# Expert blocks of a decoder's routed layer: separate PSUM tiles, one product moved, a table split over four slots

## The chip, the cores and the metric

The kernel runs on one core of a Trainium2 chip. The metric is the device time of one execution in microseconds (us), lower is better. The profiles name the engines PE (TensorE's matmuls), PEld (its weight loads), DVE (VectorE), ACT (ScalarE), POOL (GpSimd) and SP (SyncE, which issues most loads).

## The reference

Two decoder layers over x of 32 batches x 100 rows x 256 columns, with a context of 361 rows a batch and 16 heads. Each sub-layer is followed by a residual and a layer norm:

```python
x = _layernorm(x + _L0_attn_ref(x, ...))            # self-attention, softmax
x = _layernorm(x + _L0_xattn_ref(x, ctx, ctx, distances, ...))   # cross-attention, bias -log(distance)
x = _layernorm(x + _L0_ffn_ref(x, ...))             # layer norm, quantised rows, rounded weights
x = _layernorm(x + _L1_attn_ref(x, ...))
x = _layernorm(x + _L1_xattn_ref(x, ctx, ctx, ...))
x = _layernorm(x + _L1_ffn_ref(x, ...))
```

The change is in the last one, a layer of 8 experts in which each of the 3200 rows takes one:

```python
logits = x_flat @ Wg + bg
probs = softmax(logits); assignments = argmax(probs)
h = gelu(x_flat @ W1[e] + b1[e])        # for the assigned expert e
out = probs[e] * (h @ W2[e] + b2[e])
```

## The kernel before

**Slots.** Both layers' attention is written as one list of slots, five to a batch (`SLOTS`). `at(slot, place, do)` puts work into a slot; `run_slots` goes through the slots in order and emits first the scores of the step two slots ahead, then at three places the turning of the next step's probabilities with the side work of that place, and last the sums. The engines' order is the order in which this is written; nothing is rearranged later.

**Expert blocks.** While the second layer's cross-attention runs, each row's expert is found and the row is written to a region of its expert in DRAM (`regions`, values, the probability and the row's place). The regions are then handled in 32 blocks of 128 rows (`BLOCKS`), each block of one expert. A table says where each block's rows begin and whose they are. A block takes these steps:

- load its rows (`load_rows_of_block`, L112) and its expert's first matrix with bias (`load_matrix_of_block`, L115), from SP's queue;
- `turn_rows` (L117): two transposes on TensorE (L119) and one copy to SBUF on ScalarE (L120);
- `first_matrix` (L122): eight matmul passes (L126), then two activations on ScalarE with the bias (L128);
- `second_matrix` (L130): the second product (L132) from weights that stay in SBUF (`shared`), in a bank of the pool `ps_r` (four banks);
- `share_and_residual` (L135): four DVE instructions, bias, share and residual, mean and variance (L138 to L142);
- on POOL `margin` (L145) and `scale` (L148, power -0.5), on DVE `shift_of` (L151), for two blocks at a time;
- a normalisation on ScalarE (L1035) and an indirect store of the rows from POOL's queue (L779, `store`).

**Six begun blocks.** Six of the 32 blocks (`BEGUN`) are begun ahead: after 24 of the 32 batches their table is made (`table_of_begun`, L823), SP reads it (`begun_rows`), and rows are turned and first products computed in the last slots of the attention. `BEGINNING` lists for each block the (slot, place) of the turning and of the first product. They stop short of Gelu (`AF.Identity`), because ScalarE still holds the table of functions of the attention. After the last slot comes the load of the Gelu table, `table_of_others` (L836, it counts rows per expert and makes the other blocks' table on DVE, with a matmul at L801), `end_begun` (L880, Gelu at L883 and the second product of the six blocks) and `sum_begun`.

The begun blocks' table is 16 DVE instructions behind one matmul: `blocks_of_experts` (L797: count of blocks and its running sum, L803 to L809), four instructions for the whole blocks per expert (L827 to L830), `write_table` (L812, up to the transpose L821) and three for the other blocks' table (L832 to L834). All of it is emitted at slot `last + 15`, which is 313, at place 1. In that region of slots the DVE also has each pair's maximum rows (L379) and subtraction (L382) of the self-attention, and the division of a cross-attention's output (L350, L352).

**The loop.** The other 26 blocks run in a pipelined loop (L1047 to L1079). Iteration i emits: the load of block i+10, the turning of block i+2, the first product of block i+1 (now with Gelu), the normalisation of block i-3, the second product and the sum of block i, then margin and scale or shift, and the store of block i-3. Rows have 16 buffers, first matrices 12, the turned rows in SBUF (`bxT`) and the hidden rows (`bhT`) two each. In PSUM, the turned rows of block i+2 go to bank i%2 and the first product of block i+1 to bank 2 + (i+1)%2 of one tile, `sc_blocks`, of four banks. It has the shape of the attention's tile of scores and comes from the same pool, `ps_s`:

```python
banks = score_banks("blocks")          # one [P, 4, 512] tile for all blocks
turn_rows(t, banks[:, i % 2, :NC2 * P]...)
first_matrix(t, banks[:, 2 + i % 2, :NC2 * P]..., AF.Gelu)
```

Of the kernel before, what the change touches and what calls it, by code (L numbers as in the profile page):

```python
# [10 lines left out]
F32 = mybir.dt.float32  # L11
I32 = mybir.dt.int32
AF = mybir.ActivationFunctionType
# [5 lines left out]
E = 8  # L19
# [13 lines left out]
BLOCKS_AT_MOST = E * PER_EXPERT + E - 1  # L33
FILLS = 23
BEGUN, BEGIN_WITH = 6, 24
BEGINNING = (((338, 1), (340, 2)), ((338, 3), (342, 1)), ((339, 1), (343, 3)), ((339, 3), (345, 2)), ((340, 1), (346, 0)), ((341, 1), (347, 1)))
NO_TOKEN = 1000000
ROUND = 12582912.0
AHEAD = range(2, 10)
# [27 lines left out]
def decoder_kernel(ctx: ExitStack, tc: tile.TileContext, a: dict, out: bass.AP):  # L67
# [85 lines left out]
    def centre_and_scale(dst, src, scale):  # L153
        nc.vector.tensor_scalar(dst, src, scale[0], scale[1], ALU.subtract, ALU.mult)

    ps_s = ctx.enter_context(tc.tile_pool(name="ps_s", bufs=1, space=bass.MemoryType.PSUM))
    ps_r = ctx.enter_context(tc.tile_pool(name="ps_r", bufs=4, space=bass.MemoryType.PSUM))

    def bank(tag):
        return ps_r.tile([P, 512], F32, tag="r", name=f"r_{tag}")  # L160

    def score_banks(tag):
        return ps_s.tile([P, NG, 512], F32, tag="s", name=f"sc_{tag}")

    with ExitStack() as att:
        w1 = att.enter_context(tc.tile_pool(name="w1", bufs=1))
        w2 = att.enter_context(tc.tile_pool(name="w2", bufs=2))
        sm = att.enter_context(tc.tile_pool(name="sm", bufs=4))
        att.enter_context(tc.manual_schedule())

        def split(t, n):
            return t.rearrange("p (n s) -> p n s", n=n)
# [285 lines left out]
        def at(slot, place, do):  # L458
            plan.setdefault((slot, place), []).append(do)
# [337 lines left out]
        def blocks_of_experts(name, offset, before):  # L797


            ps = bank(name)[:, :E]  # L800
            nc.tensor.matmul(ps, lhsT=share_of_block, rhs=sofar, start=True, stop=True)  # L801
            n = sm.tile([P, E], F32, tag="tb_n", name=f"{name}_n")
            nc.vector.tensor_scalar(n, ps, offset, ROUND, ALU.add, ALU.add)  # L803
            if before is None:
                nc.vector.tensor_scalar(n, n, ROUND, None, ALU.subtract)
            else:
                nc.vector.scalar_tensor_tensor(n, n, ROUND, before, ALU.subtract, ALU.subtract)
            upto = sm.tile([P, E], F32, tag="tb_upto", name=f"{name}_upto")
            nc.vector.tensor_tensor_scan(upto, ones[:, :E], n, 0.0, ALU.mult, ALU.add)  # L809
            return n, upto  # L810
# [12 lines left out]
        def table_of_begun():  # L823

            assert BEGIN_WITH * S - E * (P - 1) > (BEGUN - 1) * P
            n, upto = blocks_of_experts("begun", 0.5 / P - 0.5, None)
            nc.vector.tensor_scalar(upto, upto, float(BEGUN), None, ALU.min)  # L827
            nc.vector.tensor_copy(done[:, 0:1], upto[:, 0:1])
            nc.vector.tensor_tensor(done[:, 1:], upto[:, 1:], upto[:, :E - 1], ALU.subtract)
            nc.vector.tensor_scalar(n, done, -float(P), float(B * S), ALU.mult, ALU.add)  # L830
            write_table("begun", upto, lambda: n, c["steps"][:, 0:1])
            nc.vector.tensor_tensor(over, done[:, 1:], done[:, :E - 1], ALU.subtract)  # L832
            nc.vector.tensor_scalar(over, over, float(P), float(B * S), ALU.mult, ALU.add)
            nc.vector.scalar_tensor_tensor(first_done, done[:, 0:1], float(P), c["steps"][:, 0:1], ALU.mult, ALU.add)  # L834

        def table_of_others():  # L836

# [29 lines left out]
        def of_bank(name):  # L867
            return split(bank(name)[:, :NC2 * P], NC2)

        def plan_beginning():  # L870
            last = starts(1, BEGIN_WITH - 1)[0]
            at(last + 15, 1, table_of_begun)
            at(last + 22, 3, begun_rows)
            at(last + 48, 3, begun_experts)
            for i, (turning, first) in enumerate(BEGINNING):
                at(last + 23 + i, 0, lambda i=i: load_begun(i))
                at(*turning, lambda i=i: turn_rows(blocks[i], of_bank(f"bt_{i}")))
                at(*first, lambda i=i: first_matrix(blocks[i], of_bank(f"bh_{i}"), AF.Identity))

        def end_begun():  # L880

            for t in blocks[:BEGUN]:
                nc.scalar.activation(t["hT"], t["hT"], AF.Gelu)  # L883
                t["ps"] = bank("bo")[:, :D]
                second_matrix(t, t["ps"], shared)

# [103 lines left out]
    with ExitStack() as moe:  # L990
        mw = moe.enter_context(tc.tile_pool(name="mw", bufs=1))
        m2 = moe.enter_context(tc.tile_pool(name="m2", bufs=2))
        m4 = moe.enter_context(tc.tile_pool(name="m4", bufs=4))
        m16 = moe.enter_context(tc.tile_pool(name="m16", bufs=16))
        m12 = moe.enter_context(tc.tile_pool(name="m12", bufs=12))
        moe.enter_context(tc.manual_schedule())

        y_all = mw.tile([P, BLOCKS - BEGUN, D], F32, name="y_all")
        for i in range(BEGUN, BLOCKS):
            blocks[i]["y"] = y_all[:, i - BEGUN, :]  # L1000

        banks = score_banks("blocks")

        def load_block(i):
            n = min(4, BLOCKS - i)
            if (i - BEGUN) % 4 == 0:
                firsts = of_table(i - BEGUN, n, 0, (ENG.SP,), (BLOCKS_AT_MOST - 1) * P)
                experts = of_table(i - BEGUN, n, 1, (ENG.SP, ENG.PE, ENG.DVE), E - 1)
                for t, first, e in zip(blocks[i:i + n], firsts, experts):
                    t["first"], t["e"] = first, e  # L1010
            t = blocks[i]
            t["x"] = m16.tile([P, ROW], F32, tag="xb", name=f"xb_{i}")
            t["w"] = m12.tile([P, WROW], F32, tag="wb", name=f"wb_{i}")
            for load in (load_matrix_of_block, load_rows_of_block) if i == BEGUN else (load_rows_of_block, load_matrix_of_block):
                load(t)

        def turn_block(i):
            t = blocks[i]
            t["ident"] = ident
            t["xT"] = m2.tile([P, NC2, P], F32, tag="bxT", name=f"bxT_{i}")  # L1020
            turn_rows(t, banks[:, i % 2, :NC2 * P].rearrange("p (k s) -> p k s", k=NC2))

        def first_layer(i):
            t = blocks[i]
            t["hT"] = m2.tile([P, NC2, P], F32, tag="bhT", name=f"bhT_{i}")
            first_matrix(t, banks[:, 2 + i % 2, :NC2 * P].rearrange("p (k s) -> p k s", k=NC2), AF.Gelu)

        def second_layer(i):
            ps = bank(f"bo_{i}")[:, :D]
            second_matrix(blocks[i], ps, shared)  # L1030
            share_and_residual(i, ps, m4)

        def normalise_on_scalar(i):
            y = blocks[i]["y"]
            nc.scalar.activation(y, y, AF.Identity, bias=shift[:, i:i + 1], scale=rs_all[:, i:i + 1])  # L1035

        def normalise(i):
            y = blocks[i]["y"]
            centre_and_scale(y, y, (mv_all[:, i, 0:1], rs_all[:, i:i + 1]))

        def store(i):
            scatter("out", out=out.rearrange("b s d -> (b s) d"),
                    out_offset=bass.IndirectOffsetOnAxis(ap=blocks[i]["x"][:, D + 1:].bitcast(I32), axis=0), in_=blocks[i]["y"],
                    bounds_check=B * S - 1, oob_is_err=False)

        half = BEGUN // 2
        for i in range(BEGUN - 10, BLOCKS):  # L1047
            for f, d in ((load_block, 10), (turn_block, 2), (first_layer, 1)):
                if BEGUN <= i + d < BLOCKS:
                    f(i + d)  # L1050
            if i == BEGUN - 1:
                for j in range(half):
                    normalise_on_scalar(j)
                    store(j)
            if i < BEGUN:
                continue
            if i > BEGUN + 2:
                normalise_on_scalar(i - 3)
            second_layer(i)
            if i == BLOCKS - 1:  # L1060
                normalise_on_scalar(i - 2)
                store(i - 3)
            if i == BEGUN + 1:
                margin(half, half)
                scale(half, half)
            if i % 2:
                margin(i - 1, 2)
                scale(i - 1, 2)
            elif i > BEGUN:
                shift_of(i - 2, 2)  # L1070
            if BEGUN + 1 < i < BEGUN + 2 + half:
                normalise(i - 2 - half)
                store(i - 2 - half)
            if BEGUN + 2 < i < BLOCKS - 1:
                store(i - 3)
        store(BLOCKS - 3)
        for i in range(BLOCKS - 2, BLOCKS):
            normalise(i)
            store(i)  # L1079
# [70 lines left out]
```

## Time and profile before

| | us |
|---|---|
| median of 3 runs | 1764.14 (1762.48 to 1765.47) |
| profiled execution | 1761.08 |
| its span in the trace | 1759.0 |
| start of the six second products | 1659.50 |
| second product of block 7 / 29 | 1676.64 / 1740.25 |
| one block of the loop | 2.88 |

The mean granted TensorE clock of the profiled execution is 0.995 of full speed. Positions are microseconds from the start of the span. A row of a timeline has its start, its duration, engine, line, operation, output and input tiles, shape and count; a bracket behind it is the time that the engine stood idle ahead of it, and what ended that. Up to about 1657 the profile shows the attention and what is done beside it; the expert stage is the last 100 us.

### The profile page before, as it was taken

How to read it: one execution, taken by the hardware profiler on the slowest of the kernel's cores; microseconds unless marked ns; L12 is line 12 of the kernel's file. 1: busy time of each engine (PE TensorE's matmuls, PEld its weight loads, DVE VectorE, ACT ScalarE, POOL GpSimd, SP SyncE). 2: the span in 40 equal slices, each digit the busy share in tenths (PEclk: the TensorE clock that was granted, in tenths of full speed). 3: DMA queues.
4: the chain of work that ended last, by engine and by line, in shares of the span. 5: the costliest groups of instructions: out<-in, count | busy, mean ns of one | idle time of the engine just before them, and what ended most of it. 6: DMA issues, size and time to landing. Idle time of an engine off the chain costs nothing.

```text
span 1759.0 us, 52227 instructions
## 1 busy us (share of the span) xinstructions
PE 1689.9 (96%) x20803; PEld 1298.5 (74%) x20803; DVE 1295.7 (74%) x3803; ACT 913.0 (52%) x2255; POOL 1096.0 (62%) x1655
## 2 busy tenths in 40 slices
PE   8999999999999999999999999999999999999885
PEld 6677777777777777766777777777777777776664
DVE  5677777777777777777668787877777777867754
ACT  3455555555555555555445555555555555554443
POOL 1565666666666666666157777676767676675455
PEclk9999999999999999999999999999999999999998
DMA  4000331333133213200511131000001000120261
GB/s 159 14 25 27 81 84 46 82 81 83 49 84 81 77 51 84 76 25 22 186 44 55 55 107 60 13 26 19 20 18 28 19 26 13 44 81 13 70 217 41
DMA packets 64047, 104.90 MB, mean 60 GB/s; under 512 B 6107, under 2 KB 43485, under 8 KB 63678
## 3 DMA queue, kind: packets, MB, share of 16 engines
q1 hardware_dynamic: 59790, 94.44, 18.3%
q0 software_dynamic: 3584, 6.59, 1.2%
q8 instruction: 165, 2.70, 0.6%
q14 instruction: 76, 0.62, 0.1%
q10 hardware_dynamic: 432, 0.54, 0.1%
HBM read 61.32 MB, written 41.13 MB: 58 GB/s over the span
## 4 chain that ended last, share of the span: by engine, by line
PE 76%; DVE 15%; POOL 4%; issue 3%; DMA 1%; ACT 1%; SPq 0%; POOLq 0%; ACTq 0%; DVEq 0%
PE r_t_x L435 13%; PE sc_x L341 10%; PE r_k L536 8%; PE r_v L545 7%; PE r_a_x L450 6%; DVE pr L421 6%; PE r_t_s L392 4%; PE r_o_x L364 3%; POOL pr L425 3%; PE r_qx L321 2%; PE r_o_s L364 2%; PE sc_s L341 2%; PE r_a_s L399 2%; DVE pr_s L382 2%; DVE mx_s L379 2%
## 5 line engine op out<-in xcount | busy, mean ns | idle before, releaser
L425 POOL TENSOR_TENSOR pr<-pr,mx_x 100x361 f32<-100x361 f32 x992 | 766.2, 802 | 229.4 <-DVE mx_x L421 220.2
L436 ACT ACTIVATE pT_x<-r_t_x 120x400 f32<-120x400 f32 (+1 forms) x768 | 371.0, 503 | 269.5 <-PE r_t_x L435 267.2
L435 PEld LDWEIGHTS r_t_x<-ident,pr 100*120 100x120 f32 (+1 forms) x3072 | 313.8, 138 | 111.6 <-POOL pr L425 32.8
L435 PE MATMUL r_t_x<-ident,pr 100*120 100x100 f32 (+1 forms) x3072 | 380.8, 252 | 11.8 <-POOL pr L425 10.8
L421 DVE CUSTOM_DVE_ANT_0 pr<-sc_x,dist 100x361 f32<-100x361 f32 x512 | 244.7, 531 | 121.7 <-PE sc_x L341 97.7
L421 DVE CUSTOM_DVE_ANT_0 pr<-sc_x,zero 100x361 f32<-100x361 f32 x512 | 244.6, 530 | 76.4 <-PE sc_x L341 70.3
L341 PE MATMUL sc_x<-kT_x,qz_x 32*100 32x361 f32 x2048 | 221.8, 502 | 7.8 <-DVE mx_x L421 4.5
L96 POOL TENSOR_SCALAR rs_s<-mv_s 100x1 f32<-100x1 f32 x64 | 14.3, 223 | 292.3 <-DVE mv_s L94 261.7
L450 PE MATMUL r_a_x<-pT_x,v_cross 120*32 120x100 f32 (+1 forms) x6144 | 172.2, 252 | 0.0
L379 DVE TENSOR_REDUCE mx_s<-sc_s 100x16 f32<-100x1600 f32 x64 | 116.6, 1822 | 70.8 <-PE sc_s L341 70.8
L538 ACT ACTIVATE kT_x<-r_k,c_columns 128x361 f32<-128x361 f32 x128 | 72.0, 563 | 161.8 <-PE r_k L536 161.8
L450 PEld LDWEIGHTS r_a_x<-pT_x,v_cross 120*32 120x32 f32 (+1 forms) x6144 | 129.9, 110 | 24.4 <-ACT kT_s L485 2.2
L393 ACT ACTIVATE pT_s<-r_t_s 100x400 f32<-100x400 f32 x256 | 112.5, 504 | 28.8 <-PE r_t_s L392 26.3
L382 DVE TENSOR_TENSOR pr_s<-sc_s,mx_s 100x1600 f32<-100x1600 f32 x64 | 116.8, 1825 | 2.2
L392 PE MATMUL r_t_s<-ident,pr_s 100*100 100x100 f32 x1024 | 106.2, 249 | 0.3 <-DVE pr_s L382 0.3
L341 PEld LDWEIGHTS sc_x<-kT_x,qz_x 32*100 32x100 f32 x2048 | 68.2, 159 | 44.6 <-issue 16.1
L545 PE MATMUL r_v<-shared,ctx 128*120 128x256 f32 (+1 forms) x384 | 100.5, 384 | 0.0
L392 PEld LDWEIGHTS r_t_s<-ident,pr_s 100*100 100x100 f32 x1024 | 94.3, 129 | 5.5 <-ACT shared L547 0.6
L547 ACT COPY v_cross<-r_v 120x256 f32<-120x256 f32 x168 | 62.5, 372 | 58.0 <-PE r_v L545 58.0
L332 DVE SCALAR_TENSOR_TENSOR qz_x<-r_qx,qm_x_scale,qm_x_bias 128x400 f32<-128x400 f32 x64 | 37.6, 630 | 70.1 <-PE r_qx L321 70.1
L536 PE MATMUL r_k<-ctx,c_l1x_wk 128*128 128x361 f32 x256 | 89.1, 470 | 0.1
L536 PE MATMUL r_k<-ctx,shared 128*128 128x361 f32 x256 | 88.6, 468 | 0.0
(254 smaller groups left out, 2912.7 us busy)
## 6 DMA issues: line engine op xcount, KB each, us to landing
regions<-no_token SPq DMA_DIRECT2D x23, 1161.0 KB
ctx<-in_ctxT_dram SPq DMA_DIRECT2D x64, 361.0 KB
wb<-in_experts_dram SPq DMA_DIRECT2D x26, 257.0 KB
values_dram<-shared SPq DMA_DIRECT2D x8, 768.0 KB
v_cross<-values_dram SPq DMA_DIRECT2D x8, 768.0 KB
dist<-in_dist_dram SPq DMA_DIRECT2D x32, 141.0 KB
xb<-regions SPq DMA_DIRECT2D x26, 129.0 KB
x_all<-in_x_dram SPq DMA_DIRECT2D x32, 100.0 KB
```

The costliest lines, as they stand in the source:

```text
L341: nc.tensor.matmul(dst, lhsT=qz[rows, p, k, :], rhs=kT[rows, k, :], start=True, stop=True)
L379: nc.vector.tensor_reduce(mx, sg, AX.X, ALU.max)
L382: nc.vector.tensor_tensor(pr, sg, mx.unsqueeze(3).to_broadcast([S, NG, NG, S]), ALU.subtract)
L392: nc.tensor.transpose(pt[:, j, :], t["pr_s"][:, j, g, :], ident[:S, :S])
L393: nc.scalar.activation(t["pT_s"][:, g], pt, AF.Exp)
L421: nc.vector.tensor_tensor_reduce(pr[:, j, :SK], sc[:, j, :], bias, 1.0, LOWEST, ALU.add, ALU.max, mx)
L425: nc.gpsimd.tensor_tensor(pr[:, j, :SK], pr[:, j, :SK], mx.to_broadcast([S, SK]), ALU.subtract)
L435: nc.tensor.transpose(pt[:n, j, :], t["pr_x", g][:, j, k0:k0 + n], ident[:S, :S])
L436: nc.scalar.activation(t["pT_x", g][:n, i], pt[:n], AF.Exp)
L450: nc.tensor.matmul(av[32 * j:32 * j + 32, h, :], lhsT=t["v_x"][:n, i, head(part, j), :], rhs=t["pT_x", part][:n, i, j, :], start=(i == 0), ...
L536: nc.tensor.matmul(ps, lhsT=c[sx + "_wk"][:, k, m * P:(m + 1) * P], rhs=t["ctx"][:, k, :], start=(k == 0), stop=(k == NC2 - 1))
L545: nc.tensor.matmul(ps, lhsT=ctx_b[:, k, k0:k0 + n], rhs=c[sx + "_wv"][:, k, :], start=(k == 0), stop=(k == NC2 - 1))
```

## The change

Three things change; the instructions and their number stay.

1. In the loop, each block's turned rows and each block's first product get a PSUM tile of their own, of half a bank, from a new pool `ps_m` with two buffers for each of the two kinds. In the program as built these four tiles lie in four banks, where the one tile was. The pool of the scores is closed with the attention.
2. The first product of the sixth begun block (`BEGINNING[5]`), which had slot 347, place 1, is now written in `end_begun` behind the Gelu of the first block, ahead of the six second products. On TensorE it comes right behind the matmul of the counting (L801); on ScalarE its two biased copies come behind the first Gelu.
3. `table_of_begun` returns four parts (count, whole blocks, rows of the table, the part for the other blocks), which are put at place 3 of the slots 313 to 316 instead of all at place 1 of slot 313.

```diff
-BEGINNING = (..., ((340, 1), (346, 0)), ((341, 1), (347, 1)))
+BEGINNING = (..., ((340, 1), (346, 0)), ((341, 1), None))
...
-    ps_s = ctx.enter_context(tc.tile_pool(name="ps_s", bufs=1, space=bass.MemoryType.PSUM))
...
+        ps_s = att.enter_context(tc.tile_pool(name="ps_s", bufs=1, space=bass.MemoryType.PSUM))
...
         def table_of_begun():
-            n, upto = blocks_of_experts("begun", 0.5 / P - 0.5, None)
-            nc.vector.tensor_scalar(upto, upto, float(BEGUN), None, ALU.min)
...
+            u = {}
+            def counts():
+                u["n"], u["upto"] = blocks_of_experts("begun", 0.5 / P - 0.5, None)
+            def whole_blocks():
+                n, upto = u["n"], u["upto"]
+                nc.vector.tensor_scalar(upto, upto, float(BEGUN), None, ALU.min)
+                nc.vector.tensor_copy(done[:, 0:1], upto[:, 0:1])
+                nc.vector.tensor_tensor(done[:, 1:], upto[:, 1:], upto[:, :E - 1], ALU.subtract)
+                nc.vector.tensor_scalar(n, done, -float(P), float(B * S), ALU.mult, ALU.add)
+            def rows():
+                write_table("begun", u["upto"], lambda: u["n"], c["steps"][:, 0:1])
+            def for_others():
...
+            return counts, whole_blocks, rows, for_others
...
-            at(last + 15, 1, table_of_begun)
+            for i, part in enumerate(table_of_begun()):
+                at(last + 15 + i, 3, part)
...
-                at(*first, lambda i=i: first_matrix(blocks[i], of_bank(f"bh_{i}"), AF.Identity))
+                if first:
+                    at(*first, lambda i=i: first_matrix(blocks[i], of_bank(f"bh_{i}"), AF.Identity))
...
         def end_begun():
-            for t in blocks[:BEGUN]:
+            for i, t in enumerate(blocks[:BEGUN]):
                 nc.scalar.activation(t["hT"], t["hT"], AF.Gelu)
+                if i == 0:
+                    first_matrix(blocks[BEGUN - 1], of_bank("bh"), AF.Identity)
                 t["ps"] = bank("bo")[:, :D]
                 second_matrix(t, t["ps"], shared)
...
+        ps_m = moe.enter_context(tc.tile_pool(name="ps_m", bufs=2, space=bass.MemoryType.PSUM))
...
-        banks = score_banks("blocks")
...
-            turn_rows(t, banks[:, i % 2, :NC2 * P].rearrange("p (k s) -> p k s", k=NC2))
+            turn_rows(t, ps_m.tile([P, NC2, P], F32, tag="t", name=f"bt_{i}"))
...
-            first_matrix(t, banks[:, 2 + i % 2, :NC2 * P].rearrange("p (k s) -> p k s", k=NC2), AF.Gelu)
+            first_matrix(t, ps_m.tile([P, NC2, P], F32, tag="h", name=f"bh_{i}"), AF.Gelu)
```

More of the change, by code (lines that the diff above doesn't have):

```diff
@@ L35 @@
 BEGUN, BEGIN_WITH = 6, 24
-BEGINNING = (((338, 1), (340, 2)), ((338, 3), (342, 1)), ((339, 1), (343, 3)), ((339, 3), (345, 2)), ((340, 1), (346, 0)), ((341, 1), (347, 1)))
+BEGINNING = (((338, 1), (340, 2)), ((338, 3), (342, 1)), ((339, 1), (343, 3)), ((339, 3), (345, 2)), ((340, 1), (346, 0)), ((341, 1), None))
 NO_TOKEN = 1000000
@@ L160, in bank @@
         return ps_r.tile([P, 512], F32, tag="r", name=f"r_{tag}")
-    def score_banks(tag):
-        return ps_s.tile([P, NG, 512], F32, tag="s", name=f"sc_{tag}")
     with ExitStack() as att:
@@ L168, in decoder_kernel, with score_banks @@
         sm = att.enter_context(tc.tile_pool(name="sm", bufs=4))
+        ps_s = att.enter_context(tc.tile_pool(name="ps_s", bufs=1, space=bass.MemoryType.PSUM))
         att.enter_context(tc.manual_schedule())
+        def score_banks(tag):
+            return ps_s.tile([P, NG, 512], F32, tag="s", name=f"sc_{tag}")
         def split(t, n):
@@ L825, in table_of_begun @@
             assert BEGIN_WITH * S - E * (P - 1) > (BEGUN - 1) * P
-            n, upto = blocks_of_experts("begun", 0.5 / P - 0.5, None)
-            nc.vector.tensor_scalar(upto, upto, float(BEGUN), None, ALU.min)
[L828 to L834, printed above, removed]
+            u = {}
[10 more added lines that the diff above has]
+            def for_others():
+                nc.vector.tensor_tensor(over, done[:, 1:], done[:, :E - 1], ALU.subtract)
+                nc.vector.tensor_scalar(over, over, float(P), float(B * S), ALU.mult, ALU.add)
+                nc.vector.scalar_tensor_tensor(first_done, done[:, 0:1], float(P), c["steps"][:, 0:1], ALU.mult, ALU.add)
+            return counts, whole_blocks, rows, for_others
         def table_of_others():
```

## The prediction, written before the changed kernel ran

> **What bounds the kernel now.** One run is profiled: 1761.08 us, of which the span is 1759.0. I read the page's top first:
>
> ```profile
> PE 1689.9 (96%) x20803; PEld 1298.5 (74%) x20803; DVE 1295.7 (74%) x3803; ACT 913.0 (52%) x2255; POOL 1096.0 (62%) x1655
> ```
>
> TensorE is busy 96% over all stages, but the change is in one stage and one slot, so then TensorE's timeline in the expert loop and where the loop starts, then the chain, ScalarE's timeline and the turned rows' tile to see who holds whom. In the loop one block is three rows, each ring closing with the next block's L132:
>
> ```profile
> 1720.10 1.03 PE L132 MATMUL r_bo<-shared,bhT 128*128 x4
> 1721.03 0.44 PE L119 MATMUL sc_blocks<-ident,xb 128*128 128x128 f32 x2
> 1721.99 1.16 PE L126 MATMUL sc_blocks<-bxT,wb 128*128 128x128 f32 x8 [0.52 <-ACT bxT L120]
> 1722.98 1.03 PE L132 MATMUL r_bo<-shared,bhT 128*128 x4
> ```
>
> Start, duration, line, tiles; the bracket is TensorE's idle time before the row and what ended it. From second product to second product is 2.88 us. TensorE idles 0.52 of it, for ScalarE's copy of the rows that it has just turned. But the first product (L126) is that of block i+1 and the rows are those of block i+2: nothing it reads is late. All turned rows and first products live in one tile, so an access to one orders the next. ScalarE:
>
> ```profile
> 1720.35 0.62 ACT L128 ACTIVATE bhT<-sc_blocks,wb 128x128 f32<-128x128 f32 x2 [1.30 <-PE sc_blocks L126]
> 1720.87 0.60 ACT L1035 ACTIVATE y_all<-y_all,shift,rs_all 128x256 f32<-128x256 f32 x1
> 1721.56 0.37 ACT L120 COPY bxT<-sc_blocks 128x256 f32<-128x256 f32 x1
> ```
>
> The tile's own sum says that this is the usual case (us, times):
>
> ```profile
>   ACT bxT L120: 27.9, 44
>   PE sc_blocks L126: 22.1, 17
> ```
>
> The chain has the same ring in every block: 1.16 first product, 0.87 second, 0.35 turning, 0.38 copy. The other engines have room in 1716 to 1728 (12 us): DVE 6.62, ScalarE 6.11, POOL 6.46. Where the stage starts, TensorE shows:
>
> ```profile
> 1657.77 0.43 PE L801 MATMUL r_counts<-sofar,share_of_block 100*128 100x8 f32 x2
> 1659.50 8.03 PE L132 MATMUL r_bo<-shared,x_all 128*128 x24 [1.31 <-ACT x_all L883]
> 1667.37 0.38 PE L119 MATMUL sc_blocks<-ident,xb 128*128 128x128 f32 x2
> ...
> 1672.82 1.16 PE L126 MATMUL sc_blocks<-bxT,wb 128*128 128x128 f32 x8 [1.28 <-ACT x_all L1035]
> 1673.81 1.03 PE L132 MATMUL r_bo<-shared,bhT 128*128 x4
> ```
>
> After the counting it waits 1.31 us for Gelu, then needs 8.03 us for six second products that take 24 x 0.2155 = 5.2 us at full clock. The stretches tell why (length, busy time of TensorE, its weight loads, DVE, ScalarE and POOL, then the granted clock, here 0.50 and 0.81, DMA share, GB/s):
>
> ```profile
> 1662.00:1664.00 2.00, 2.00 (x6) 1.55 (x6) 1.78 (x6) 0.00 (x0) 0.00 (x0) 0.50 0.56 159
> 1664.00:1666.00 2.00, 2.00 (x9) 1.70 (x8) 1.83 (x6) 0.00 (x0) 0.00 (x0) 0.81 0.90 249
> ```
>
> It is half from 1657.93 for 6.83 us. Lastly, the begun blocks' table on DVE, first and last of its rows and who waits behind:
>
> ```profile
> 1527.94 0.16 DVE L803 TENSOR_SCALAR begun_n<-r_begun 128x8 f32<-128x8 f32 x1
> ...
> 1530.36 0.15 DVE L834 SCALAR_TENSOR_TENSOR first_done<-done,c_columns 128x1 f32<-128x1 f32 x1
> ...
> 1531.00 0.42 DVE L352 TENSOR_TENSOR o_x<-r_n_x,rc_x 100x256 f32<-100x256 f32 x1
> ```
>
> **Loop: tiles of their own.** No instruction is added or removed. In the order that the built program has, turning waits only for its rows' load, the first product for the copy made an iteration before and the load of its matrix, and the second product for the Gelu of its own block and for the DVE add four blocks back. So the 0.52 goes, and also the turning's wait for the Gelu. What is late next is TensorE itself: first product to second 0.99 (1719.11 to 1720.10), second to turning 0.93 (1720.10 to 1721.03), turning to first product now 0.96, of which 0.52 is idle. That leaves 0.44 at most; the nearest row where nothing waits behind a turning (a begun block, 1643.68 to 1643.90) has 0.22. Period: 2.14, or 2.36 at most; I take 2.14, since that row is the same turning with a TensorE instruction ready behind it. From the second product of block 7 (1676.64) to that of block 29 (1740.25) are 22 periods of 2.89. At 2.14 they gain 22 x 0.75 = 16.5, at 2.36 11.7.
>
> The cover holds, but not everywhere by much. ScalarE has 0.37 + 0.62 + 0.60 = 1.59 a block, DVE 1.6, POOL 3.57 a pair (margin, power, two stores, 1720.01 to 1723.58) or 1.8 a block. The tightest is the shift: it ends 2.75 after the second product ahead of it (1714.35, 1717.09), and its normalisation's turn on ScalarE comes 0.77 after the next one, now at 2.91. It is 0.16 early; if that is gone the normalisation waits, and the next copy behind it, which is needed only an iteration later. Loads: 390 KB a block land every 1.3 us from 1664 to 1682 and stay ahead of 2.14. Behind the second product of block 29 the end is the same string of POOL steps as before, so it is moved and keeps its length.
>
> **Start: first product behind the counting.** Eight passes leave the slot at 1655.92, where they cost nothing: the next TensorE step waits for DVE (hot) until 1657.39. They now stand between the counting and the second products. At half clock a pass of 128 columns is 0.22 (twice 0.11), so 1658.0 to 1659.8, in the old 1.31 idle but for the last 0.3, by which the second products start later. ScalarE's two biased copies of block 5 stand between Gelu of block 0 and of block 1 (0.63), ahead of need; no second table load, as the loop has Identity among its Gelus without one. Then two ends. If the half clock ends after half of the 6.83 (at 1661.34), the second products take four passes at 0.427 and 20 at 0.2155 and end at 1665.8; rows 6 have landed (1665.1). Turning 6 and 7 stand ahead of first product 6 (1666.6), turning 8 1667.6, first product 7 1667.85, and first product 8 waits for its copy behind three normalisations (shift of the first three at about 1668.5, so until 1670.2): second product 7 at 1671.25, not 1676.64, a gain of 5.4. If the half clock lasts as long as now, the second products end at 1667.4 and the same steps end at 1673.05: 3.6. No row tells between them; I take the middle, 4.5.
>
> [...]
>
> **Table in four slots.** The period of the self-attention's maximum rows that holds the table is 26.92 us, its counterpart without one (1425.94 to 1450.38) 24.44: the table costs 2.5 on the path. Its 16 DVE instructions (1527.94 to 1530.51, 2.57) stand ahead of L350 and L352, and o_x comes 6.66 after the maximum (1524.34 to 1531.00), in the counterpart 4.18 (1425.94 to 1430.12): the same 2.5. In four slots, at the last place, the matmul of the count (0.31) stays; 0.6 of counting delays one L421; the four instructions of whole blocks (0.65) fit a DVE gap of 0.85, the three of the last part (0.45) one of 1.35; the transposed table (about 1.0) stands where the counterpart had 0.8 free. That is 0.35 to 1.2 kept, a gain of 1.3 to 2.1, taken as 1.7; at worst, if every slot is full, it is nothing. SP reads the table's addresses five slots behind the part that writes them, and no DMA moves on SP's or POOL's queue.
>
> **Sum.** 16.5 + 4.5 + 1.7 = 22.7, from 1761.08 to 1738.4. The profiled run is 3.06 under the median of 1764.14, so the median becomes 1741.4.
>
> **Rivals.**
> First: the loop is freed, but not down to TensorE's own 2.14: weight loads that now lie in the idle time show, or POOL's stores run late, and with them shift and normalisation. For: the 0.16 of slack, and six begun stores ahead of the loop's on POOL. Against: POOL idles 2.18 a pair. Period 2.36: 11.7 + 4.5 + 1.7 = 17.9, so 1746.2; with the start at 3.6 and the table at 0.5, 1748.3.
>
> Second: the waits do not go, as the new tiles still order each other. Against: the built order. [...] The loop stays at 2.89; the table's 1.7 and up to 1.8 of clock are left: 1760.6 to 1764. [...]
>
> Third, slower: the pairs become one string, DVE 1.63, margin and power 1.02 with 0.2 to the next, two normalisations 1.2, two stores 2.35, 6.4 a pair or 3.2 a block, when the normalisation holds up ScalarE's copies and TensorE waits for these. It starts at the three normalisations ahead of first product 8, so the start gains nothing: 22 x 0.31 = 6.8 lost, 1.7 gained, 1769.2. It decides once the shift is later than the copies have slack, 0.16 plus about 2 us. Against: three blocks of distance between product and normalisation, in which two pairs are under way.
>
> **How the numbers follow.** Forecast 0.63, first rival 0.25, second 0.06, third 0.04; 0.02 for a gain beyond the forecast's best, 5.4 + 16.5 + 2.1 = 24.0 or 1740.1. The range takes forecast and first rival: from 1737.5 (2.6 under that best, for the spread of medians of about 1.5 and a first product overlapping better) to 1749.0. What a measurement here can tell from no change is 0.2%, 3.5 us: faster below 1760.6, which forecast and first rival are and the second's best just reaches. Faster 0.92, same 0.04, slower 0.04.
>
> **What would show it.** Loop: TensorE rows L132, L119, L126 without a bracket, 2.14 apart; a bracket naming ACT bxT would refute it, one naming y_all or shift is the first or third rival. Start: no 1.31 after the counting; second product 7 at 1671 to 1673 less the table's gain; half clock 3.4 or 6.8 long. Table: the period of maximum rows that was 26.92 at about 25.2. Wrong would be a period over 2.4, or an end behind block 29 longer than now, 18.8 us to the span's end.

## The result, and the profile after

The changed kernel takes 1736.53 us, median of six runs (1733.78 to 1737.63), against 1764.11 for the kernel before (1761.33 to 1766.09). The ratio is 0.9843, with a 95% interval from 0.9831 to 0.9856, so 27.6 us are gained. The prediction was 1741.4 with a range from 1737.5 to 1749.0: the direction and the places were right, the gain was larger than said, and the median lies 1 us under the range. The profiled execution took 1733.78 with a span of 1731.8.

TensorE's timeline in the loop, after (start, duration, line, operation, tiles, count):

```profile
1691.31 1.03 PE L132 MATMUL r_bo<-shared,bhT 128*128 x4
1692.17 0.38 PE L119 MATMUL bt<-ident,xb 128*128 128x128 f32 x2
1692.39 1.06 PE L126 MATMUL bh<-bxT,wb 128*128 128x128 f32 x8
1693.29 1.03 PE L132 MATMUL r_bo<-shared,bhT 128*128 x4
```

No bracket is left, and a block is 1.98 long: 0.90 from first product to second product, 0.86 to the turning, 0.22 to the next first product. The stretch of twelve microseconds shows the same (length; busy time of TensorE, weight loads, DVE, ScalarE, POOL; granted clock, DMA share, GB/s):

```profile
1686.00:1698.00 12.00, 12.00 (x86) 11.06 (x86) 9.49 (x28) 8.59 (x25) 10.10 (x14) 1.00 0.87 265
```

TensorE is the bound, its weight loads 92% busy and POOL 84%. Where the stage starts:

```profile
1655.61 0.37 PE L801 MATMUL r_counts<-sofar,share_of_block 100*128 100x8 f32 x2
1655.83 1.25 PE L126 MATMUL r_bh<-x_all,xnT 128*128 128x128 f32 x8
1656.88 6.99 PE L132 MATMUL r_bo<-shared,x_all 128*128 x24
1663.71 0.60 PE L119 MATMUL bt<-ident,xb 128*128 128x128 f32 x4
...
1668.26 1.16 PE L126 MATMUL bh<-bxT,wb 128*128 128x128 f32 x8 [0.29 <-ACT bxT L120]
1669.25 1.03 PE L132 MATMUL r_bo<-shared,bhT 128*128 x4
```

The 1.31 us idle behind the counting is filled by the moved product, and second product 7 follows the counting after 13.64 us (1655.61 to 1669.25) instead of 18.87. The granted clock in stretches of two microseconds (third number from the right):

```profile
1656.00:1658.00 2.00, 2.00 (x11) 1.82 (x11) 1.72 (x12) 1.60 (x6) 0.99 (x1) 0.68 0.00 0
1658.00:1660.00 2.00, 2.00 (x7) 1.56 (x6) 1.26 (x5) 1.27 (x5) 0.00 (x0) 0.50 0.18 52
1660.00:1662.00 2.00, 2.00 (x11) 1.77 (x10) 1.85 (x6) 0.00 (x0) 0.00 (x0) 0.97 0.69 190
```

It is half for 3.4 us in all, not for 6.8. And DVE around the first two parts of the table:

```profile
1528.13 0.42 DVE L352 TENSOR_TENSOR o_x<-r_n_x,rc_x 100x256 f32<-100x256 f32 x1
...
1530.02 0.15 DVE L803 TENSOR_SCALAR begun_n<-r_begun 128x8 f32<-128x8 f32 x1
...
1532.75 0.75 DVE L833 TENSOR_SCALAR begun_upto<-begun_upto 128x8 f32<-128x8 f32 x1
```

The division's o_x now comes 4.17 after its pair's maximum (1523.96), like the counterpart's 4.18, and the table's parts stand in later gaps. The period that holds the table is 25.17, not 26.92.

So the spans' 27.2 us are made up as follows:

| | before | after | gain | forecast |
|---|---|---|---|---|
| span's start to the counting | 1657.77 | 1655.61 | 2.16, of it 1.75 the table | 1.7 |
| counting to second product 7 | 18.87 | 13.64 | 5.23 | 4.5 |
| second product 7 to 29 | 63.61 | 43.81 | 19.80 | 16.5 |
| second product 29 to the end | 18.75 | 18.74 | 0.01 | 0 |

### The profile page after: what moved, and what is told of

It is laid out like the page before. It is cut to its first block, busy times and chain, and to the rows that moved or that the text cites. A ratio compares the mean times of both kernels' runs of the same rounds, so it can differ in the third digit from the quotient of the medians.

```text
span 1731.8 us, 52249 instructions
## 1 busy us (share of the span) xinstructions
PE 1678.4 (97%) x20803; PEld 1298.7 (75%) x20803; DVE 1296.1 (75%) x3803; ACT 911.9 (53%) x2255; POOL 1096.8 (63%) x1655
## 4 chain that ended last, share of the span: by engine, by line
PE 78%; DVE 14%; POOL 3%; issue 2%; DMA 1%; ACT 0%; POOLq 0%; SPq 0%; DVEq 0%; ACTq 0%
PE r_t_x L435 13%; PE sc_x L341 10%; PE r_k L536 8%; PE r_v L545 7%; PE r_a_x L450 6%; DVE pr L421 6%; PE r_t_s L392 4%; PE r_o_x L364 3%; POOL pr L425 3%; PE r_o_s L364 3%; PE r_qx L321 3%; PE sc_s L341 2%; PE r_a_s L399 2%; DVE pr_s L382 2%; DVE mx_s L379 2%
```

## Experiments

Two questions were open: which part brings how much, and why a block takes 1.98 and not 2.14.

| run | median | ratio to before | interval |
|---|---|---|---|
| tiles only | 1737.23 | 0.9850 | 0.9832 to 0.9867 |
| moved product only | 1764.90 | 1.0004 | 0.9994 to 1.0015 |
| table only | 1764.23 | 1.0000 | 0.9990 to 1.0010 |
| tiles and table | 1736.49 | 0.9851 | 0.9831 to 0.9871 |
| two shared tiles | 1740.54 | 0.9862 | 0.9840 to 0.9884 |
| tiles by parity | 1743.77 | 0.9880 | 0.9858 to 0.9902 |
| rows turned late | 1757.50 | 0.9958 | 0.9946 to 0.9969 |
| ten matmuls in the gap | 1738.82 | 0.9854 | 0.9832 to 0.9877 |
| change again | 1737.78 | 0.9852 | 0.9828 to 0.9875 |
| tiles again | 1739.75 | 0.9858 | 0.9833 to 0.9882 |
| five matmuls in the gap | 1735.35 | 0.9839 | 0.9816 to 0.9861 |

### The parts alone

Tiles only: the kernel before with part 1 of the diff.

> Only the tiles of their own (part 1). Theory A (the one tile's false waits held TensorE, and each wait cost more than the idle time that the trace printed: about 0.1 in the first product and 0.07 behind the second): the loop runs at 1.98 to 2.0 us a block as in the changed kernel, block 7 to block 29 takes 43.8, the start keeps its long half clock and gains about 3.5, the whole 22 to 24 us under before. Theory B (the loop's shorter rows need the other parts too, through a loop that starts sooner or in another clock phase): 2.14 a block, 16 us plus the start.

The trace has 1.98 a block and 43.81 from second product 7 to 29, the changed kernel's own numbers. The counting to second product 7 takes 14.97, with the long half clock: 3.9 of the start's gain come from the tiles by themselves. This is theory A. The median of 1737.23 is 26.9 under before's 1764.16 in these runs, more than the 22 to 24 expected, while the two traces' spans differ by 23.9 (1759.0 and 1735.1). So the tiles bring nearly all of the change's gain.

Moved product only: the kernel before with part 2.

> Only the first product of block 5 moved behind the counting (part 2). Theory A: the loop stays at 2.89; TensorE has no 1.31 us idle behind the counting, the half clock ends one stretch of 3.4 us earlier, and the six second products end 1.5 earlier: 0 to 1.8 us under before. Theory B (the half clock does not depend on that idle time): the second products start 0.3 later and nothing is gained, 0 to 0.5 over before.

The median is 1764.90, no difference that can be told from zero. In its trace the counting to second product 7 takes 18.39 instead of 18.87, and the half clock is 6.8 us long although the idle time behind the counting is filled: in this execution it begins at 1659.7, ahead of the counting (1660.85), in the gaps before it. Theory A's 1.5 is not there; 0.5 is.

Table only: the kernel before with part 3.

> Only the begun blocks' table in four slots (part 3). Theory A: the period of the maximum rows that holds the table falls from 26.92 to 25.17, as in the changed kernel, and nothing else changes: 1.75 us under before. Theory B (part of that was lent by the other parts): under 1 us.

The period is 25.17 as expected, 1.75 saved, but the median is that of before; its interval reaches just to the 1.75 (0.9990). The trace's own time, 1766.01, is even longer, since it runs at half clock in three places where the profiled execution of before does not. They are the subject of the clock experiments below.

Tiles and table: the changed kernel without part 2.

> The changed kernel with the first product of block 5 back in its slot (parts 1 and 3). Theory A: loop 1.98, table 25.17, but the 1.31 idle behind the counting is there again and the half clock is 6.8 long: second product of block 7 about 1.5 us later against the counting, the whole 1 to 1.8 us over the changed kernel. Theory B (clock independent of the moved product): within 0.5 of the changed kernel.

The median, 1736.49, is 0.7 under the tiles alone and no higher than the changed kernel's 1736.53, where theory A expected 1 to 1.8 more. The idle time behind the counting is back, but the half clock is 3.4 long all the same; the counting to second product 7 takes 13.98. Against the changed kernel's 13.64 the moved product is worth 0.3 when the stretches fall like this, and 1.3 against the 14.97 of the tiles alone.

### What the tile's sharing cost

Two shared tiles:

```diff
-        ps_m = moe.enter_context(tc.tile_pool(name="ps_m", bufs=2, space=bass.MemoryType.PSUM))
+        ps_m = moe.enter_context(tc.tile_pool(name="ps_m", bufs=1, space=bass.MemoryType.PSUM))
...
+        turned = ps_m.tile([P, 2, 512], F32, tag="t", name="turned")
+        hidden = ps_m.tile([P, 2, 512], F32, tag="h", name="hidden")
...
-            turn_rows(t, ps_m.tile([P, NC2, P], F32, tag="t", name=f"bt_{i}"))
+            turn_rows(t, turned[:, i % 2, :NC2 * P].rearrange("p (k s) -> p k s", k=NC2))
...
-            first_matrix(t, ps_m.tile([P, NC2, P], F32, tag="h", name=f"bh_{i}"), AF.Gelu)
+            first_matrix(t, hidden[:, i % 2, :NC2 * P].rearrange("p (k s) -> p k s", k=NC2), AF.Gelu)
```

> The changed kernel with one two-bank tile for all turned rows and one two-bank tile for all first products, in place of a tile for each block. Theory A (only the mixing of the two kinds in one tile made false waits: the copy and the Gelu of an iteration before are long done when their own kind comes again): 1.98 us a block, no idle time that names the copy, the same time as the changed kernel. Theory B (each block needs a tile of its own): idle time behind the Gelu or the copy comes back, 2.1 to 2.9 a block, 3 to 20 us over the changed kernel.

The result lies between the two theories. Most blocks take 1.98, as theory A says, so the false waits come from mixing rows and products in one tile. But in eight of the 22 periods something is late, and second product 7 to 29 takes 48.83, 5.0 more. Such a place, on ScalarE and then on TensorE:

```profile
1692.81 0.62 ACT L128 ACTIVATE bhT<-hidden,wb 128x128 f32<-128x128 f32 x2 [1.39 <-PE r_bo L132]
```

```profile
1693.49 1.16 PE L126 MATMUL hidden<-bxT,wb 128*128 128x128 f32 x8 [0.55 <-ACT bhT L128]
```

The Gelu starts 1.2 us behind the last pass of its product (1691.58), where 0.36 is usual, and the next first product, which shares its tile, has to wait for it. With a tile for each block it would not. What held up that Gelu the trace doesn't settle; the kernel with own tiles has some late Gelus too (0.60 for block 17), at no cost. The runs (1740.23 to 1740.83) all lie above the changed kernel's (1733.78 to 1739.27, change again included), so two shared tiles are slower; that the 5.0 in the loop is lateness passed on, and not lateness of their making, is read from rows like these and not shown apart.

Tiles by parity:

```diff
+        halves = [ps_m.tile([P, 2, 512], F32, tag="p", name=f"half_{j}") for j in range(2)]
...
-            turn_rows(t, ps_m.tile([P, NC2, P], F32, tag="t", name=f"bt_{i}"))
+            turn_rows(t, halves[i % 2][:, 0, :NC2 * P].rearrange("p (k s) -> p k s", k=NC2))
...
-            first_matrix(t, ps_m.tile([P, NC2, P], F32, tag="h", name=f"bh_{i}"), AF.Gelu)
+            first_matrix(t, halves[i % 2][:, 1, :NC2 * P].rearrange("p (k s) -> p k s", k=NC2), AF.Gelu)
```

> The changed kernel with one two-bank tile for the even blocks and one for the odd blocks, turned rows and first product of a block together. The first product then waits for no copy but its own, yet the turning of block i+2 has to wait for the Gelu of block i, which was the second false wait of before. Theory A: that wait ends about when the second product ahead of it does, so it costs 0 to 0.1 a block: 1.98 to 2.08, and the copy's wait was nearly the whole of the 0.9 a block. Theory B (the Gelu's wait was half of the loss): 2.3 to 2.5.

```profile
1690.30 1.03 PE L132 MATMUL r_bo<-shared,bhT 128*128 x4
1691.22 0.44 PE L119 MATMUL half<-ident,xb 128*128 128x128 f32 x2
1691.50 1.06 PE L126 MATMUL half<-bxT,wb 128*128 128x128 f32 x8
```

The usual block takes 2.10, and second product to turning is 0.92 again, as in before (0.93), with 0.28 to the first product instead of 0.22. The turning waits for the Gelu of two blocks earlier, which costs 0.12 a block, and in the usual block no bracket shows it. So the copy's wait was nearly the whole of the 0.9, as theory A says. Late steps cost more than this here too (2.4 to 3.6 in six periods): of the 6.2 by which second product 7 to 29 is longer, the 0.12 makes 2.6.

Rows turned late:

```diff
-            for f, d in ((load_block, 10), (turn_block, 2), (first_layer, 1)):
+            for f, d in ((load_block, 10), (turn_block, 1), (first_layer, 1)):
```

> The changed kernel with the rows of block i+1 turned in iteration i, not those of block i+2: the first product right behind now waits for its own copy, a true wait in the place of the false one, with the tiles of the changed kernel. Theory A (a TensorE that has waited also shows the weight load of its next pass, about 0.1, which the idle time in the trace does not count): first product to second product 0.99 again, turning to first product 0.96, second product to turning 0.87: 2.8 a block. Theory B (the 0.1 came from the shared tile itself): 0.89 instead of 0.99, 2.7 a block.

```profile
1693.06 0.38 PE L119 MATMUL bt<-ident,xb 128*128 128x128 f32 x2
1693.96 1.16 PE L126 MATMUL bh<-bxT,wb 128*128 128x128 f32 x8 [0.52 <-ACT bxT L120]
1694.96 1.03 PE L132 MATMUL r_bo<-shared,bhT 128*128 x4
```

This is the row of before, made by a true wait with tiles of their own. First product to second product is 1.00 again, not 0.90. The turning starts 0.86 behind the second product (1692.20 to 1693.06), since it waits for no Gelu, and the period is 2.76. This is theory A: behind the wait of 0.52, the first product takes 0.10 more with tiles of its own too. In the single passes of before, the first of the eight after the wait starts 0.21 ahead of the second (1721.99 and 1722.20), and the others are 0.11 apart; the weight load of that first pass starts with it, at 1721.99. In the changed kernel, without a wait, it starts 0.11 ahead of its pass (1692.28 and 1692.39), under the pass before.

### The clock

The kernel before, profiled once more.

> The kernel before, profiled once more. Theory A (the profiled execution of before was short of the median because stretches at half clock of 3.4 us, which cost up to 1.7 us each, fall in some executions at about 75, 908 and in the first 20 us of the expert loop and in others do not): this trace has at least one such stretch more, and its time differs from 1761.1 by about 1.6 for each. Theory B (the spread between executions comes from transfers): same stretches, another time.

Its execution took 1765.66. Two stretches in its loop's start, and the second of them in the first profile of before, in the same columns as above:

```profile
1672.00:1676.00 4.00, 2.95 (x11) 2.50 (x12) 0.79 (x3) 1.83 (x5) 2.64 (x3) 0.50 1.00 318
1676.00:1680.00 4.00, 3.48 (x13) 2.67 (x12) 1.52 (x4) 0.86 (x3) 1.56 (x3) 0.50 1.02 350
```

```profile
1676.00:1680.00 4.00, 3.48 (x25) 2.84 (x24) 1.99 (x6) 1.23 (x4) 1.38 (x3) 1.00 0.99 351
```

The same kernel at the same place runs at half clock for 10 us in one execution and at full clock in the other. There are also 3.4 us at 907 to 911, which lengthen one period of the maximum rows by 1.62. From the counting to second product 29 it takes 85.23 instead of 82.48. The two make 4.4 of the 4.6 us by which the spans differ (1759.0 and 1763.6). The table alone had the same stretch in its loop (86.47), one at 909 to 912 and one more at 75. What TensorE does ahead of that one is the same with and without it; table alone first, then the changed kernel:

```profile
72.00:75.00 3.00, 2.04 (x21) 1.22 (x19) 1.87 (x9) 1.29 (x3) 2.57 (x4) 1.00 0.06 16
75.00:79.00 4.00, 3.55 (x58) 3.25 (x61) 1.74 (x8) 1.75 (x4) 3.49 (x5) 0.59 0.38 123
```

```profile
72.00:75.00 3.00, 2.04 (x20) 1.17 (x18) 1.87 (x9) 1.30 (x3) 2.61 (x4) 1.00 0.08 8
75.00:79.00 4.00, 3.56 (x78) 2.72 (x78) 1.92 (x9) 2.03 (x5) 3.45 (x5) 1.00 0.39 129
```

With 2.04 busy of 3.00 in both, the clock halves in one execution and not in the other. This is theory A: one kernel's executions differ by whole stretches. What decides whether a stretch falls at such a place was not shown: TensorE was busy for 1.64 of the 3.41 us ahead of the stretch at 907, and no run shows how much idle time it takes.

The change and the tiles alone once more, timed beside each other.

> The changed kernel again, timed beside the tiles alone. [...] Theory B (parts 2 and 3 are given back before the end): within 0.7 of the tiles alone.

> The tiles alone again (part 1), beside the run of the whole change. Theory A: 1 to 3.3 us over the changed kernel; loop 1.98 a block; in the trace the period with the table 26.92 and a half clock of 6.8 behind the counting. Theory B: within 0.7 of it.

1737.78 and 1739.75: the two small parts bring 2.0 in the medians, inside the expected 1 to 3.3, though the two kernels' runs overlap (1736.75 to 1739.27 and 1737.14 to 1741.22). The traces have 25.18 against 26.92 for the period with the table, and 13.60 against 14.41 from the counting to second product 7. In both, the loop has one late block of 2.75 and 2.77.

Ten matmuls of the identity in the gap ahead of the places' products, to see whether the half clock behind the counting comes from the idle time ahead of it:

```diff
+WARM = (347, 1)
...
+        def warm():
+            ps = of_bank("warm")
+            for k in range(10):
+                nc.tensor.matmul(ps[:, k % NC2, :], lhsT=ident, rhs=ident, start=True, stop=True)
...
+            at(*WARM, warm)
```

> The changed kernel with ten passes of the identity by itself added in slot 347, place 1, where TensorE waits 1.33 us for DVE ahead of the places' products; their result is not used. [...]

The trace has no half clock up to the last blocks. But each matmul is two passes in the trace (x20), ten take 2.3 us and make the products of the places 0.8 late, and one block of the loop takes 3.57: 1738.82, nothing gained. Five of them, with `range(5)`:

> The changed kernel with five matmuls of the identity by itself in the gap ahead of the places' products (ten passes, 1.1 us, where ten matmuls took 2.2 and delayed the products by 0.8); their result is not used. Theory A (clock by idle time): no or a short half clock behind the counting, second products 5.2 to 6, the places' products not delayed; the gain is 0 to 0.7 us, as the turning of block 6 then waits for its rows. Theory B (clock fixed otherwise): 7.0 for the second products, no change.

```profile
1653.86 1.36 PE L885 MATMUL r_warm<-ident 128*128 128x128 f32 x10
...
1656.90 5.77 PE L133 MATMUL r_bo<-shared,x_all 128*128 x24
1663.45 0.86 PE L120 MATMUL bt<-ident,xb 128*128 128x128 f32 x4 [0.78 <-DMA xb<-regions]
```

The half clock behind the counting is gone and the six second products take 5.77 instead of 6.99. All twelve traces without such matmuls have 3.4 or 6.8 us of half clock there, and neither of the two with them has any. So in the changed kernel it does come from the idle time ahead of it, 1.33 us in front of the places' products, as theory A says. TensorE then waits 0.78 for the rows of block 6, and second product 7 comes 13.34 behind the counting instead of 13.64. The median, 1735.35, is 2.4 under that of the changed kernel timed beside it, but the five runs reach from 1733.49 to 1739.38 and overlap it; the trace accounts for 0.3 only. It is the lowest median here and not shown to be faster than the change.

## Why the prediction was right and wrong

**The loop.** The waits went as said, and TensorE became the bound. The step that failed is the term of the period: "first product to second 0.99", "second to turning 0.93", taken for TensorE's own time. Both belonged to a TensorE that had waited. They are 0.90 and 0.86 without: 0.10 is the weight load that shows behind a wait (rows turned late), 0.07 the turning's wait for the Gelu, too short for a bracket (tiles by parity). The 0.22 was right. The prediction saw that the Gelu's wait would go, and gave it no price. At 1.98 instead of 2.14 the 22 periods bring 3.5 more; one late block (2.28) gives back 0.3. That is 3.3 of the 4.5 by which the trace's gain exceeds the forecast of 22.7. The rest is 0.7 of the start, which lies between its two ends, and 0.5 ahead of the counting.

**The range.** Its lower end was made from the same 2.14, with only 2.6 under the best sum for the spread of medians and a first product that overlaps better; the loop's shorter blocks alone bring 3.5. The rows for a bound were there: eight passes 0.11 apart, four at 0.2155 and 0.22 for the turning are 1.96.

**The first rival** is real, but small: 0.3 us in this trace. The begun blocks' stores delay POOL, the shift waits for it, and ScalarE's copy stands behind the normalisation; POOL, DVE, ScalarE and TensorE of the changed kernel:

```profile
1681.20 0.98 POOL L779 DMA_INDIRECT out_dram<-y_all,xb  x1 [0.30 <-ACT bxT L120]
1682.18 0.26 POOL L145 TENSOR_SCALAR rs_all<-mv_all 128x2 f32<-128x2 f32 x1
```

```profile
1683.27 0.16 DVE L151 SCALAR_TENSOR_TENSOR shift<-mv_all,rs_all 128x2 f32<-128x2 f32 x1 [1.33 <-POOL rs_all L148]
```

```profile
1683.47 0.60 ACT L1049 ACTIVATE y_all<-y_all,shift,rs_all 128x256 f32<-128x256 f32 x1 [1.48 <-DVE shift L151]
```

```profile
1683.96 0.38 PE L119 MATMUL bt<-ident,xb 128*128 128x128 f32 x2
1684.38 1.16 PE L126 MATMUL bh<-bxT,wb 128*128 128x128 f32 x8
1685.38 1.03 PE L132 MATMUL r_bo<-shared,bhT 128*128 x4
```

First product 16 then starts 0.2 late and in the old way, with 1.00 to the second product. It happens once: the normalisation's later waits for the shift are shorter (0.84, then 0.48). Three more traces of the same loop have one such block of 2.70 to 2.77, so up to 0.8. The change again, ScalarE and TensorE:

```profile
1686.48 0.60 ACT L1049 ACTIVATE y_all<-y_all,shift,rs_all 128x256 f32<-128x256 f32 x1 [1.95 <-DVE shift L151]
```

```profile
1687.39 1.16 PE L126 MATMUL bh<-bxT,wb 128*128 128x128 f32 x8 [0.51 <-ACT bxT L120]
```

The second and the third rival are out: the built order's waits were gone in the trace, and no string of pairs formed.

**The start** gained 5.23, near the upper end, with one stretch of half clock. That end, 5.4, took the half clock to last half of the 6.83; no run had shown that length when the prediction was written, and the changed kernel's trace shows it (3.4). But the prediction put the start's gain down to the moved product, and 3.9 of it come with the tiles alone. Nor does the moved product alone decide how long the half clock is. In the twelve traces without added matmuls, the stretch at the counting is with it 3.4 long in four of six and 6.8 in two (moved product only, rows turned late), without it 3.4 in two of six (tiles and table, before again) and 6.8 in four. Its share is 0.3 to 1.3 in the traces, and in the median of the moved product alone nothing can be told from zero.

**The table** gave 1.75 for 1.7, in the traces with part 3. In a total it is nowhere clear of the noise: nothing by itself, and 0.7 beside the tiles.

**From trace to median** the profiled execution's distance of 3.06 was carried over, and the changed kernel's is 2.75. For before a second trace shows what it is mostly made of: stretches at half clock which the first profiled execution happens not to have. For the change they are only a part: its second profiled execution (1736.75) is 3.0 longer than the first, of which 1.62 is a stretch at half clock at 908 to 911, 0.86 falls in the first 21 us and 0.47 in the loop's late block.

## What to carry to other kernels

Where an engine's idle time is to be removed, take its own pace from rows in which it never waited, or from the spacing of single passes; rows right behind a wait were longer here than without one, by 0.16 on a block of 1.98, and a range needs a bound on that side too. One tile for two kinds of data made the one wait for the other here (0.52 idle in a block of 2.88); kinds in tiles of their own took the steady wait away (1.98), and a tile for each block cost 5.0 us less in the loop here than two shared ones. A part that saves 1 to 2 us where executions differ by steps of 1.6 is judged from its place in the trace, not from the median alone.

## What was not expected of the hardware

The granted clock halved although TensorE had been busy for half to three quarters of the 3.4 us ahead (1.64 of 3.41 ahead of 907.4 in before again, 2.45 of 3.42 ahead of 1657.9 in before) and had been idle for 1.81 us at most at a time in these two, in some executions and not in others at the same place. The stretches ahead of the last blocks are 3.4 us long, or two or three times that (6.8 in before, 10 in before again); the one at 907 cost 1.62. Ten passes put into a gap of 1.33 us went with a full clock behind the counting, in the one trace that has them.
